# Idle products moved into TensorE's small gaps, and the third block's scores moved behind the sum over w1, in a gated cross-attention and feed-forward kernel

## The chip, the cores and the metric

The kernel runs on one core of a Trainium2 chip. The metric is the time of one execution on the device, in microseconds, lower is better; several runs are taken and their median is shown. A profile of one execution comes beside it, and its "span" runs from the first to the last instruction of that execution.

## The reference

Inputs are x (4 blocks of 512 rows of 512), a context ctx (4 blocks of 512 rows of 128), two gates, one attention vector W of 256 numbers with its bias b, and three weights of 1408 x 512 (w1, w2) and 512 x 1408 (w3).

```python
# attention part, per block
si = ctx @ W[:128];  sj = ctx @ W[128:]
att = 0.6 * sigmoid(si[:, None] + sj[None, :] + b) + 0.4 * layernorm(x)
x = x + tanh(g_xattn) * att
# feed-forward part, on layernorm(x)
bitlinear(v, w) = quant8(rmsnorm(v)) @ quant_ternary(w).T
x = x + tanh(g_ffn) * bitlinear(silu(bitlinear(h, w1)) * bitlinear(h, w2), w3)
```

`quant_ternary` divides a weight by the mean of its absolute values, rounds and clips to -1, 0, 1. So a weight can be rounded only when the sum of |w| over the whole weight is known. `quant8` scales each row by its largest absolute value.

## The kernel before

The 2048 rows are 16 tiles of 128 rows, numbered 0 to 15; a block (batch entry) has four of them. Each tile goes through: scores and tanh (attention), layer norm, rounding to 8 bits, a turn on TensorE (`pt`, line 419), the unloading of the turned tile (`un`, line 427 on ScalarE or 429 on VectorE), products with w1 (`G`, the gates, `pg` in the trace) and with w2 (`U`, `pu`), silu (`SI`), the product of both (`ST`), its largest value (`AM`), rounding, another turn, products with w3 (`D`, `po`), and the write.

Nothing schedules the work: the string `ORDER` (line 33) lists the steps, and each engine runs its own instructions in that order. An instruction that waits holds up all that follows on its engine. A digit after a step is its tile, block or weight, `.k` a part of it, and the last letter the engine (a ScalarE, v VectorE, p GpSimd). The steps that matter here:

- `bp2` and the like (`spread_param`, line 196): a one-row product that spreads a scalar over the partitions; `up` (line 202, 204) reads it. `bp1` spreads the attention gate, from whose tanh `cg` (line 217 to 222, VectorE) makes the constants that the layer norm scale needs.
- `pi b` (line 315): the row scores of block b, four products of one column, each with a load of its own; `si b` (line 327, ScalarE) reads them. `pj b` (line 322): the column scores, one product of 512 columns in 32-bit floats.
- `wu n` (`keep_busy`, line 180): n products of 128x512 whose result, the tile `idle`, nobody reads.
- `A1.k`, `A2.k`: sums of |w| of part k on ScalarE (line 242) or VectorE (line 244). `tot1`, `tot2` (line 248): TensorE adds the parts over the partitions. `M1`, `M2` (lines 253 to 256, VectorE): mean and its inverse. `R` (lines 264, 266): the weight is scaled and rounded; `C` (line 269): it is clipped into the f16 weight that the products read. The tiles between `R` and `C` have three buffers.
- The scores, `tot`, `pt` and the spread scalars all take turns in two PSUM buffers (`ps_o`, tag "po"), in program order: each new one waits until the one two places before it has been read.

At the start, in program order and before `ORDER` begins: DMAs of the parameters, constants (`ones`, `mhalf`, the identity), the tile `ones16` of ones on GpSimd, three idle products, and then `bc` (lines 185 and 186), which spreads W over the partitions and is copied to `wc` by ScalarE (line 188). The scores need `wc`.

Of the kernel before, what the change touches and what calls it, by code (L numbers as in the profile page):

```python
# [11 lines left out]
F16 = mybir.dt.float16  # L12
# [8 lines left out]
P = 128  # L21
# [11 lines left out]
ORDER = """  # L33
x0 ctx0 x3 x2 x1 ctx1 w1.0 w1.1 w1.2 w1.3 ctx2 ctx3 w2.0 w2.1 w2.2 w2.3 x10 w3.0 x4 x6 x8 w3.1 w3.2
x14 x12 st0 bp1 up1 cg cc st3 bp0 up0 pi0 si0 st2 pj0 th2 st1 la2 th0 la0 th1 pi1 lb2v at2 si1 lb0v
at0 ce0v at1 ce1v am0 an0 th3 at3 am1 an1 A1.0a A1.1a A1.2a wu4 bp2 pj1 up2 wu13 pi2 A1.3v pjs1 sq1
A1.4v si2 ce3p sq0 am3 tot1 M1 ce2p r1p r0p pt1 un1a R1.2v pt0 un0v R1.3a am2 an3 pi3 si3 an2 C1.3v
C1.2v A2.0a th7 pj2 R1.0p C1.0v A2.1a wu4 G0.0 R1.1p A2.2v A2.3a C1.1v A2.4v G1.0 G1.1 st10 tot2 M2
R2.0v G0.1 r2v sq3 sq2 r3p G0.2 G0.3 dq0 C2.0v R2.1p st11 st5 C2.1v pjs2 R2.2a C2.2v pt3 pj3 SI0
R2.3a C2.3v G1.2 lc0 G1.3 SI1 st4 st6 un3a th6 U0.0 th4 U0.1 U0.2 U0.3 ST0 U1.0 U1.1 st7 U1.2 U1.3  # L40
ST1 A3.1a dq2 pt2 un2a mr la4 lb4v th5 at4 G3.0 G3.1 G3.2 pjs3 G3.3 SI3 at5 ce5a at6 ce4v am5 G2.0
G2.1 G2.2 an5 G2.3 SI2 U3.0 U3.1 at7 am4 U3.2 ce6p an4 U3.3 ST3 ce7p U2.0 U2.1 r5p pt5 am7 sq4 sq6
an7 sq5 r4p sq7 un5a th8 r7p A3.0a am6 U2.2 U2.3 pt4 G5 ST2 st8 an6 st9 dq4 r6p AM1 AN1 th11 un4a
SI5 A3.2a U5 ST5 lc2 pt6 pt7 G4 th10 la8 lb8v at10 at8 un6a G6 at11 AM5 SI4 QU1p th9 fx3p ce10a
sq10 ce11p am11 an11 ce8p am8 an8 AN5 un7a U4 ST4 T1 r11p tot3 M3 AM2 SI6 am10 fx1p an10 AN2 sq11
W1a G7 at9 sq8 pt11 un11a SI7 r8p U6 SQ0 pt8 un8a U7 ST6 R3.1p ce9p SQ1 r10p pt10 sq9 am9 lc4 an9
os un10a ST7 st15 th15 r9p dq8 G8 SI8 th14 G11 SI11 AM0 R3.2p pt9 U8 th12 QU2p AN0 st14 st12 st13
QU0p C3.1v un9a ST8 G10 SQ7 AM8 la12 lb12v at14 th13 at13 G9 T0 ce13v SI10 AM6 lc8 fx2p R3.0a am13
an13 SI9 U11 ST11 AM7 AN7 SQ6 AM3 C3.0p T2 W2a U9 ST9 W0a AN3 at15 SQ2 ce14p r13p U10 pt13 un13a
AN6 am14 an14 C3.2p DQ0 D1 S1 QU7p at12 T7 sq14 W7a QU3p ce12v am12 ce15p SQ3 AN8 sq13 an12 am15  # L50
an15 SQ5 DQ2 G13 r15p fx7p ST10 D2 S2 SQ11 D0 sq12 fx8p AM11 fx0p S0 sq15 dq12 T3 QU6v r12p AN11
U13 W3a SI13 DQ6 lc12 ST13 fx13p QU8p pt15 r14p O2 D7 un15a S7 pt12 un12a SQ10 SQ8 AM4 G15 SI15 AN4
QU4p T6 W6v D3 S3 O3 QU5p fx9p O7 fx6p AM9 AN9 SQ13 fx14p D6 S6 T8 QU9p O1 AM10 AN10 AM13 SQ9 W8a
U15 ST15 AN13 SQ4 T5 G12 T4 fx12p W5a D5 W4a fx4a fx11p AM15 fx5a O0 fx10p SI12 DQ4 S5 DQ8 D8 S8 T9
W9a QU11p U12 ST12 AM12 O8 pt14 un14a AN12 T11 AN15 O6 QU13p O5 DQ10 W11a D4 S4 D9 fx15p T13 S9
QU12v SQ12 G14 W13a QU10v T12 W12v O9 D11 S11 D13 QU15v T10 SI14 DQ12 S13 U14 ST14 T15 AM14 AN14
SQ15 DQ15 W10a D10 S10 QU14v W15a O11 D12 S12 O12 SQ14 T14 W14a D15 DQ14 O10 O13 S15 D14 S14 O15 O4
O14
"""


# [1 line left out]
def flamingo_gated_kernel(  # L63
# [29 lines left out]
    act, dve, pool, pe, sp = nc.scalar, nc.vector, nc.gpsimd, nc.tensor, nc.sync  # L93

    const = ctx.enter_context(tc.tile_pool(name="const", bufs=1))
# [65 lines left out]
        load_param(i)  # L161


    ones = const.tile([P, P], F32, name="ones")
    dve.memset(ones, 1.0)
    mhalf = const.tile([P, TB], F32, name="mhalf")
# [4 lines left out]
    act.activation(warm, ones[:, 0:1], AF.Silu)  # L171


    ones16 = const.tile([P, 512], F16, name="ones16")
    pool.memset(ones16, 1.0)  # L175
    idle = ps_gu.tile([P, 3 * 512], F32, tag="gu", name="idle")

    def keep_busy(n):
        for _ in range(n):
            pe.matmul(idle[:, :512], ones16[:, :P], ones16, start=True, stop=True)  # L180


    keep_busy(3)
    bc = ps_o.tile([P, 512], F32, tag="po", name="bc")
    pe.matmul(bc[:, P : P + 1], row[:, :C], ones[0:1, 0:1], start=True, stop=True)
    pe.matmul(bc[:, :P], row[:, C : 2 * C], ones[0:1, :], start=True, stop=True)
    wc = const.tile([P, P + 1], F32, name="wc")
    act.activation(wc, bc[:, : P + 1], AF.Copy)
    wj, wi = wc[:, :P], wc[:, P : P + 1]
# [113 lines left out]
    am1 = const.tile(NTT, F32, name="am1")  # L303
# [267 lines left out]
    for step in ORDER.split():  # L571
        name, n, k, eng = re.fullmatch(r"([A-Za-z]+)(\d*)\.?(\d?)([apv]?)", step).groups()
# [46 lines left out]
```

## Time and profile before

| | us |
|---|---|
| median of 3 runs | 157.71 (157.62 to 158.26) |
| the profiled execution | 157.83 |
| its span | 156.1 |
| TensorE busy | 146.2 (94%) |
| VectorE busy | 126.9 (81%) |
| ScalarE busy | 118.6 (76%) |
| GpSimd busy | 97.4 (62%) |
| idle products (L180), busy | 9.0, in 24 products |

The profile has views: busy times by engine, the span in 40 slices with the granted TensorE clock, the chain of work that ended last, the groups of instructions, the waits, and the timeline of one engine. In a chain or timeline row the first number is the start in microseconds from the span's start, the second the length. A bracket at the end of a timeline row gives how long the engine stood idle just before it and what ended that. Each 32-bit product appears as two pairs of a load (PEld) and a product (PE), so the four products of `pi` are shown as x8.

### The profile page before, as it was taken

How to read it: one execution, taken by the hardware profiler on the slowest of the kernel's cores; microseconds unless marked ns; L12 is line 12 of the kernel's file. 1: busy time of each engine (PE TensorE's matmuls, PEld its weight loads, DVE VectorE, ACT ScalarE, POOL GpSimd, SP SyncE). 2: the span in 40 equal slices, each digit the busy share in tenths (PEclk: the TensorE clock that was granted, in tenths of full speed). 3: DMA queues.
4: the chain of work that ended last, by engine and by line, in shares of the span. 5: the costliest groups of instructions: out<-in, count | busy, mean ns of one | idle time of the engine just before them, and what ended most of it. 6: DMA issues, size and time to landing. Idle time of an engine off the chain costs nothing.

```text
span 156.1 us, 2167 instructions
## 1 busy us (share of the span) xinstructions
PE 146.2 (94%) x704; PEld 75.4 (48%) x704; DVE 126.9 (81%) x216; ACT 118.6 (76%) x164; POOL 97.4 (62%) x161
## 2 busy tenths in 40 slices
PE   5999969979999999999999999999999999999980
PEld 2853643535554545555455454545554545555330
DVE  1679599999999999999999999959699296748621
ACT  3269499999799999997999879689979583737300
POOL 6241569782366886589959888889998962130400
PEclk9999995999999999999999999999999999999999
DMA  4799999996000000000000000100600321010162
GB/s 118 278 425 412 432 411 421 422 404 249 1 0 0 6 0 0 0 0 0 0 4 0 0 0 0 69 4 0 247 24 0 123 79 70 1 67 0 64 249 90
DMA packets 6690, 18.21 MB, mean 117 GB/s; under 512 B 663, under 2 KB 664, under 8 KB 6424
## 3 DMA queue, kind: packets, MB, share of 16 engines
q1 hardware_dynamic: 6672, 18.09, 29.4%
q8 instruction: 5, 0.08, 0.2%
q14 instruction: 5, 0.04, 0.1%
q10 hardware_dynamic: 8, 0.00, 0.0%
HBM read 13.89 MB, written 4.19 MB: 116 GB/s over the span
## 4 chain that ended last, share of the span: by engine, by line
PE 68%; DVE 21%; ACT 3%; POOL 3%; issue 1%; DVEq 0%; POOLq 0%; ACTq 0%
PE pg L459 19%; PE pu L459 18%; PE po L526 15%; PE idle L180 5%; DVE hs L471 5%; DVE f_am L483 5%; PE pj L322 3%; PE pi L315 3%; DVE x L366 2%; PE qp L419 2%; DVE x L531 2%; DVE am L388 2%; ACT junk L396 1%; DVE q L411 1%; PE pt L419 1%
## 5 line engine op out<-in xcount | busy, mean ns | idle before, releaser
L459 PEld LDWEIGHTS <-ht 128*128 128x128 f16 x384 | 37.7, 99 | 38.5 <-issue 3.5
L459 PE MATMUL pu<-w2q,ht 128*128 128x512 f16 (+1 forms) x192 | 40.4, 362 | 1.1 <-DVE w2q L269 1.1
L459 PE MATMUL pg<-w1q,ht 128*128 128x512 f16 (+1 forms) x192 | 41.1, 367 | 0.0
L526 PE MATMUL po<-w3q,qt 128*128 128x512 f16 x176 | 39.4, 379 | 0.7 <-ACT ht L427 0.4
L471 DVE SCALAR_TENSOR_TENSOR hs<-pu,a,hs 128x1408 f32<-128x1408 f32 x16 | 26.8, 1676 | 6.3 <-PE pu L459 2.4
L427 ACT ACTIVATE qt<-qp 128x1536 f16<-128x1536 int8 x14 | 20.2, 1448 | 12.9 <-PE qp L419 12.7
L526 PEld LDWEIGHTS <-qt 128*128 128x128 f16 x176 | 17.2, 98 | 20.1 <-issue 1.0
L467 ACT ACTIVATE hs<-pg,a 128x1408 f32<-128x1408 f32 x16 | 22.8, 1426 | 4.5 <-POOL a L406 2.4
L483 DVE TENSOR_REDUCE f_am<-hs 128x1 f32<-128x1409 f32 x16 | 25.7, 1609 | 0.1
L491 ACT ACTIVATE junk<-hs 128x1408 bf16<-128x1408 f32 x16 | 22.0, 1375 | 0.1
L500 POOL TENSOR_SCALAR q<-hs,f_qs 128x1024 int8<-128x1024 f32 (+1 forms) x22 | 19.2, 888 | 1.1 <-DVE f_qs L488 0.6
L531 DVE SCALAR_TENSOR_TENSOR x<-po,f_dq,x 128x512 f32<-128x512 f32 x16 | 11.9, 746 | 9.7 <-PE po L526 8.4
L345 DVE BATCH_NORM_STATS2 st<-x 128x6 f32<-128x512 f32 x16 | 10.8, 675 | 3.1 <-DMA x<-in_x_dram 3.1
L382 POOL TENSOR_SCALAR th_all<-x,ysum 128x512 f32<-128x512 f32 x9 | 6.8, 761 | 10.1 <-DVE x L366 6.6
L366 DVE SCALAR_TENSOR_TENSOR x<-x,sc,th_all 128x512 f32<-128x512 f32 x16 | 12.3, 788 | 0.7 <-ACT th_all L338 0.3
L411 POOL TENSOR_SCALAR q<-th_all,qs 128x512 int8<-128x512 f32 x15 | 10.3, 689 | 3.3 <-PE pt L419 1.4
L374 POOL TENSOR_SCALAR x<-x,c_sig,sh 128x512 f32<-128x512 f32 x14 | 11.6, 833 | 0.1
L516 POOL TENSOR_SCALAR f_w<-f_ss,kap 128x2 f32<-128x2 f32 (+1 forms) x9 | 2.4, 268 | 14.2 <-ACT junk L491 13.6
L388 DVE TENSOR_REDUCE am<-th_all 128x1 f32<-128x513 f32 x16 | 10.8, 676 | 0.0
L180 PE MATMUL idle<-ones 128*128 128x512 f16 x24 | 9.0, 534 | 1.8 <-POOL ones L175 1.8
L396 ACT ACTIVATE junk<-th_all 128x512 bf16<-128x512 f32 x16 | 10.1, 628 | 0.7
L427 ACT ACTIVATE ht<-pt 128x512 f16<-128x512 int8 x15 | 8.8, 589 | 1.9 <-PE pt L419 1.8
(94 smaller groups left out, 182.1 us busy)
## 6 DMA issues: line engine op xcount, KB each, us to landing
out_dram<-x SPq DMA_DIRECT2D x16, 256.0 KB, 2.3
x<-in_x_dram SPq DMA_DIRECT2D x6, 512.0 KB, 13.1
hs<-in_w1t_dram SPq DMA_DIRECT2D x4, 704.0 KB, 6.7
hs<-in_w2t_dram SPq DMA_DIRECT2D x4, 704.0 KB, 11.6
w3f<-in_w3t_dram SPq DMA_DIRECT2D x2, 1024.0 KB, 14.9
x<-in_x_dram SPq DMA_DIRECT2D x4, 256.0 KB, 5.1
ctx<-in_ctx_t_dram SPq DMA_DIRECT2D x4, 256.0 KB, 7.3
w3f<-in_w3t_dram SPq DMA_DIRECT2D x1, 768.0 KB
```

The lines of the kernel that those rows point to most:

```text
L180: pe.matmul(idle[:, :512], ones16[:, :P], ones16, start=True, stop=True)
L366: dve.scalar_tensor_tensor(xt(n), xt(n), col(sc, n), ths[n], ALU.mult, ALU.add, accum_out=col(ysum, n))
L388: dve.tensor_reduce(col(am1, n), th_all[:, th_slot[n], : D + 1], AX.X, ALU.max, apply_absolute_value=True)
L427: act.activation(dst, src, AF.Copy)
L459: pe.matmul(gus[tag, n][:, c0 : c0 + cn], hts[n][:, kk, :], wq[:, kk, c0 : c0 + cn], start=(kk == 0), stop=(kk == ND - 1),)
L467: act.activation(tts[n], gus.pop(("pg", n))[:, :H], AF.Silu, scale=col(a1, n))
L471: dve.scalar_tensor_tensor(tts[n], gus.pop(("pu", n))[:, :H], col(a1, n), tts[n], ALU.mult, ALU.mult)
L483: dve.tensor_reduce(col(f_am, n), hs[:, t_slot[n], : H + 1], AX.X, ALU.max, apply_absolute_value=True)
L491: act.activation(junk[:, :H], tts[n], AF.Square, accum_out=col(f_ss, n))
L500: eng.tensor_scalar(dst, src, col(f_qs, n), 127.0, ALU.mult, ALU.mult)
L526: pe.matmul(po[:, :D], qt[:, f, :], w3q[:, f, :], start=(f == 0), stop=(f == NH - 1))
L531: dve.scalar_tensor_tensor(xt(n), pos.pop(n)[:, :D], col(f_dq, n), xt(n), ALU.mult, ALU.add)
```

## The change

1. The memset of `ones16` on GpSimd stands ahead of the other constants.
2. Four idle products ahead of `bc` where there were three, and three new ones between `bc` and `bp1`.
3. In `ORDER`: `wu13 pi2` ahead of `tot1` becomes `wu12`; `pi2` and `si2` go behind `pt0`; `wu2` stands between `pt1` and `pt0`, another `wu2` between `pt0` and `pi2`, `wu3` ahead of `pj2`, and the `wu4` ahead of `G0.0` becomes `wu2`.

```diff
-at0 ce0v at1 ce1v am0 an0 th3 at3 am1 an1 A1.0a A1.1a A1.2a wu4 bp2 pj1 up2 wu13 pi2 A1.3v pjs1 sq1
-A1.4v si2 ce3p sq0 am3 tot1 M1 ce2p r1p r0p pt1 un1a R1.2v pt0 un0v R1.3a am2 an3 pi3 si3 an2 C1.3v
-C1.2v A2.0a th7 pj2 R1.0p C1.0v A2.1a wu4 G0.0 R1.1p A2.2v A2.3a C1.1v A2.4v G1.0 G1.1 st10 tot2 M2
+at0 ce0v at1 ce1v am0 an0 th3 at3 am1 an1 A1.0a A1.1a A1.2a wu4 bp2 pj1 up2 A1.3v pjs1 sq1 A1.4v
+ce3p sq0 am3 wu12 tot1 M1 ce2p r1p r0p pt1 un1a R1.2v wu2 pt0 wu2 pi2 si2 un0v R1.3a am2 an3 pi3
+si3 an2 C1.3v C1.2v A2.0a th7 wu3 pj2 R1.0p C1.0v A2.1a wu2 G0.0 R1.1p A2.2v A2.3a C1.1v A2.4v G1.0
+G1.1 st10 tot2 M2
...
+    ones16 = const.tile([P, 512], F16, name="ones16")
+    pool.memset(ones16, 1.0)
     ones = const.tile([P, P], F32, name="ones")
...
-    ones16 = const.tile([P, 512], F16, name="ones16")
-    pool.memset(ones16, 1.0)
     idle = ps_gu.tile([P, 3 * 512], F32, tag="gu", name="idle")
...
-    keep_busy(3)
+    keep_busy(4)
     bc = ps_o.tile([P, 512], F32, tag="po", name="bc")
     pe.matmul(bc[:, P : P + 1], row[:, :C], ones[0:1, 0:1], start=True, stop=True)
     pe.matmul(bc[:, :P], row[:, C : 2 * C], ones[0:1, :], start=True, stop=True)
+    keep_busy(3)
```

All that follows `M2` in `ORDER` is as before. On TensorE the instructions otherwise keep their order; on ScalarE only `si2` moves, from ahead of `sq0` to behind `un1a`, just ahead of `R1.3a`; GpSimd has the memset of `ones16` ahead of the identity; VectorE and the DMA queue keep their order. With `pi2` moved, `tot1` and `pt1` take other PSUM buffers: `tot1` now waits for `up2`, `pt1` for `pjs1`, `pi2` for `un1a`, `pi3` for `un0v`, `pj2` for `si2`.

More of the change, by code (lines that the diff above doesn't have):

```diff
@@ L35 @@
 x14 x12 st0 bp1 up1 cg cc st3 bp0 up0 pi0 si0 st2 pj0 th2 st1 la2 th0 la0 th1 pi1 lb2v at2 si1 lb0v
-at0 ce0v at1 ce1v am0 an0 th3 at3 am1 an1 A1.0a A1.1a A1.2a wu4 bp2 pj1 up2 wu13 pi2 A1.3v pjs1 sq1
-A1.4v si2 ce3p sq0 am3 tot1 M1 ce2p r1p r0p pt1 un1a R1.2v pt0 un0v R1.3a am2 an3 pi3 si3 an2 C1.3v
-C1.2v A2.0a th7 pj2 R1.0p C1.0v A2.1a wu4 G0.0 R1.1p A2.2v A2.3a C1.1v A2.4v G1.0 G1.1 st10 tot2 M2
-R2.0v G0.1 r2v sq3 sq2 r3p G0.2 G0.3 dq0 C2.0v R2.1p st11 st5 C2.1v pjs2 R2.2a C2.2v pt3 pj3 SI0
@@ L40 @@
[L40 to L57, printed above, removed]
@@ L58 @@
-O14
+at0 ce0v at1 ce1v am0 an0 th3 at3 am1 an1 A1.0a A1.1a A1.2a wu4 bp2 pj1 up2 A1.3v pjs1 sq1 A1.4v
+ce3p sq0 am3 wu12 tot1 M1 ce2p r1p r0p pt1 un1a R1.2v wu2 pt0 wu2 pi2 si2 un0v R1.3a am2 an3 pi3
+si3 an2 C1.3v C1.2v A2.0a th7 wu3 pj2 R1.0p C1.0v A2.1a wu2 G0.0 R1.1p A2.2v A2.3a C1.1v A2.4v G1.0
+G1.1 st10 tot2 M2 R2.0v G0.1 r2v sq3 sq2 r3p G0.2 G0.3 dq0 C2.0v R2.1p st11 st5 C2.1v pjs2 R2.2a
+C2.2v pt3 pj3 SI0 R2.3a C2.3v G1.2 lc0 G1.3 SI1 st4 st6 un3a th6 U0.0 th4 U0.1 U0.2 U0.3 ST0 U1.0
+U1.1 st7 U1.2 U1.3 ST1 A3.1a dq2 pt2 un2a mr la4 lb4v th5 at4 G3.0 G3.1 G3.2 pjs3 G3.3 SI3 at5 ce5a
@@ new lines @@
+at6 ce4v am5 G2.0 G2.1 G2.2 an5 G2.3 SI2 U3.0 U3.1 at7 am4 U3.2 ce6p an4 U3.3 ST3 ce7p U2.0 U2.1
+r5p pt5 am7 sq4 sq6 an7 sq5 r4p sq7 un5a th8 r7p A3.0a am6 U2.2 U2.3 pt4 G5 ST2 st8 an6 st9 dq4 r6p
+AM1 AN1 th11 un4a SI5 A3.2a U5 ST5 lc2 pt6 pt7 G4 th10 la8 lb8v at10 at8 un6a G6 at11 AM5 SI4 QU1p
+th9 fx3p ce10a sq10 ce11p am11 an11 ce8p am8 an8 AN5 un7a U4 ST4 T1 r11p tot3 M3 AM2 SI6 am10 fx1p
+an10 AN2 sq11 W1a G7 at9 sq8 pt11 un11a SI7 r8p U6 SQ0 pt8 un8a U7 ST6 R3.1p ce9p SQ1 r10p pt10 sq9
@@ new lines @@
+am9 lc4 an9 os un10a ST7 st15 th15 r9p dq8 G8 SI8 th14 G11 SI11 AM0 R3.2p pt9 U8 th12 QU2p AN0 st14
+st12 st13 QU0p C3.1v un9a ST8 G10 SQ7 AM8 la12 lb12v at14 th13 at13 G9 T0 ce13v SI10 AM6 lc8 fx2p
+R3.0a am13 an13 SI9 U11 ST11 AM7 AN7 SQ6 AM3 C3.0p T2 W2a U9 ST9 W0a AN3 at15 SQ2 ce14p r13p U10
+pt13 un13a AN6 am14 an14 C3.2p DQ0 D1 S1 QU7p at12 T7 sq14 W7a QU3p ce12v am12 ce15p SQ3 AN8 sq13
+an12 am15 an15 SQ5 DQ2 G13 r15p fx7p ST10 D2 S2 SQ11 D0 sq12 fx8p AM11 fx0p S0 sq15 dq12 T3 QU6v
+r12p AN11 U13 W3a SI13 DQ6 lc12 ST13 fx13p QU8p pt15 r14p O2 D7 un15a S7 pt12 un12a SQ10 SQ8 AM4
@@ new lines @@
+G15 SI15 AN4 QU4p T6 W6v D3 S3 O3 QU5p fx9p O7 fx6p AM9 AN9 SQ13 fx14p D6 S6 T8 QU9p O1 AM10 AN10
+AM13 SQ9 W8a U15 ST15 AN13 SQ4 T5 G12 T4 fx12p W5a D5 W4a fx4a fx11p AM15 fx5a O0 fx10p SI12 DQ4 S5
+DQ8 D8 S8 T9 W9a QU11p U12 ST12 AM12 O8 pt14 un14a AN12 T11 AN15 O6 QU13p O5 DQ10 W11a D4 S4 D9
+fx15p T13 S9 QU12v SQ12 G14 W13a QU10v T12 W12v O9 D11 S11 D13 QU15v T10 SI14 DQ12 S13 U14 ST14 T15
+AM14 AN14 SQ15 DQ15 W10a D10 S10 QU14v W15a O11 D12 S12 O12 SQ14 T14 W14a D15 DQ14 O10 O13 S15 D14
+S14 O15 O4 O14
```

## The prediction

> **What bounds the kernel now.** I read the page's 40 slices first:
>
> ```profile
> PE   5999969979999999999999999999999999999980
> ```
>
> TensorE is at 9 tenths from slice 10 to slice 38 (39 us to near the end), so a shift of the first gates and ups moves all that follows. The change ends ahead of `M2`, so the question is when `M2` and the products behind it start. Next the chain of work that ended last:
>
> ```profile
> 1.82 1.46 PE idle L180 x3
> 3.28 0.51 PE bc L185 x2
> ...
> 5.49 1.84 PE pi L315 x8
> 7.32 1.92 PE pj L322 x2
> 9.24 1.50 PE pi L315 x8
> 10.74 1.73 PE idle L180 x4
> ...
> 14.98 3.62 PE idle L180 x13
> 18.60 0.80 PE pi L315 x8
> ...
> 27.80 0.13 PE tot L248 x2
> 27.93 0.02 issue
> 27.96 0.18 DVE mean L253
> ...
> 33.59 4.32 PE pu L459 x21
> ```
>
> The chain stays on TensorE almost without a break from 1.82 to 19.4. It reaches `tot2` at 27.80 and `M2` at 27.96, and from 33.59 on TensorE is dense again. Then VectorE's timeline, for what `tot1` releases:
>
> ```profile
> 19.65 0.16 DVE L253 TENSOR_REDUCE mean<-tot 128x1 f32<-128x5 f32 x1 [1.69 <-PE tot L248]
> ...
> 22.49 1.38 DVE L269 TENSOR_SCALAR w1q<-wk 128x1408 f16<-128x1408 int16 x3
> ```
>
> VectorE stood idle 1.69 us for `tot1` and was then busy without a break up to 27.86, where `st10` ends (27.68 + 0.18). So `M2` at 27.96 is 0.10 behind VectorE's own work: TensorE's path to `tot2` is late by that 0.10 and no more. Of this stretch the order on VectorE is the bound.
>
> Third, the clock. In the stretch table the granted clock is:
>
> ```profile
> 23.00:24.00 1.00, 1.00 (x4) 0.28 (x2) 1.00 (x4) 1.00 (x3) 0.90 (x1) 0.66 1.07 416
> ...
> 26.00:27.00 1.00, 1.00 (x5) 0.40 (x3) 1.00 (x3) 0.91 (x3) 0.92 (x2) 0.63 0.89 358
> ```
>
> 0.66 and 0.63 at a floor of 0.50 put the fall at 23.32 and the return at 26.73, 3.41 us apart. The page has no record for the first 16 us and prints 9 there, but the rows speak: `wu4` at 10.74 took 1.73, 0.43 a product; the starts inside `wu13` are 0.43 apart up to 16.48 and 0.22 apart after it. So TensorE ran at half speed until 16.49, at full speed for two steps of 3.41, at half speed for one. Steps fall at 9.66, 13.08, 16.49, 19.90, 23.32, 26.73. What went through the array in each (column streams of `pj` and idle products; `pi` and `bp` stream one column): 6.25 to 9.66 1.9 us, no rise; 9.66 to 13.08 1.8 us, no rise; 13.08 to 16.49 all 3.4, rise; 16.49 to 19.90 1.9, kept; 19.90 to 23.32 about 1.0 (`pj2` alone), fall. So a rise wants somewhere between 1.9 and 3.4 us of streaming in a step, and keeping wants between 1.0 and 1.9.
>
> [...]
>
> **The change, step by step** (times of the profiled execution).
>
> 1. *`ones16` first.* GpSimd's first memset of this set starts at 0.72 and `ones16` takes 0.52, so the idle products start at 1.29 and not 1.82: 0.53 gained, and the fourth costs 0.43. `bc` comes 0.10 earlier at 3.11, or not at all earlier if the parameter row lands later (its landing isn't shown). The identity is 0.5 later; its first reader is at 19.83, so nothing.
>
> 2. *`wu3` between `bc` and `bp1`.* `bp1` needs only the gate's DMA and ran at 4.23, in the shadow of the copy to `wc`; the hole was just 4.65 to 4.80. Now three products at half speed (0.43 each) start at 4.13. A one-row load comes 0.56 behind the last idle product's start (11.83 to 12.39 at `bp2`, 2.65 to 3.21 at `bc`), so `bp1` is at 4.98 + 0.56 = 5.54 and `bp0` 0.52 behind at 6.06, where it stood at 4.80. `pi0` starts at 6.58 instead of 5.49: **+1.1 us**. All behind it follows: `pj0`, the four tanh on ScalarE, `at2` on VectorE (10.06, it waited for the tanh), the sums A1. VectorE's gate constants are 1.4 later, its statistics 0.7; they are ready ahead of the tanh. The last A1 sum ends at 17.37 + 1.1 = 18.46. The weights don't hide this: VectorE's A1 sums were not waiting for a DMA.
>
> 3. *One idle product fewer, `pi2` out of the way.* `wu12` starts at 14.78 + 1.1 = 15.88. If the clock still rises at 16.49, the second product ends at 16.61 and ten more by 0.216 end at 18.77, which is when `tot1` starts: **0.48 earlier** than 19.25, and behind the A1 sums (18.46).
>
> 4. *`pi2` and `si2` behind `pt0`.* `pt1` starts 0.2 after `tot1` (18.97), `un1a` on ScalarE 0.37 after that (19.34) and takes 0.59. On TensorE two idle products, `pt0` and two more (0.43 + 0.13 + 0.43) put `pi2` at 20.10. From `pi2` to `si2` took 0.99 (18.43 to 19.42), so `si2` is at 21.09. Behind it on ScalarE waits `R1.3a`, which ran at 20.67 and now at 21.25; it takes 1.47, and `C1.3v` on VectorE can't start before 22.75. It was at 22.49: **+0.26**. VectorE's own order would have had it 0.48 earlier, at 22.0, so the gain of step 3 turns into a wait for `R1.3a`. Behind `C1.3v` are `C1.2v`, `C1.0v`, A2.2v, C1.1v, A2.4v, `st10` and `M2`, and GpSimd's `R1.1p`, which waits for a buffer that `C1.3v` frees: all +0.26. `st10` ends at 28.12.
>
> 5. *The pairs and the clock at 23.32.* Behind `pi2` (0.85) `pi3` waits for `un0v`, which VectorE ends at 21.30, and ends at 22.2; `wu3` ends at 22.85, then `pj2`. Streaming from 19.90 to 23.32 becomes 0.2 + 0.65 + 0.47 = 1.3 us against a need between 1.0 and 1.9: open. If the clock holds, `G1.1` waits for `C1.1v`, which ends at 26.4, and `tot2` is done by 27.2. If it falls, the rest of `pj2` and `wu2` end at 25.05 and `G0.0`, `G1.0` (1.17 each at half speed) and `G1.1` bring `tot2` to 27.8. Both are ahead of 28.12, where `st10` ends: TensorE is no longer what `M2` waits for, and the 0.10 by which `tot2` was late goes, of which 0.02 of issue stays: **-0.08**. Bounds: 0 and -0.10. The held clock itself buys nothing here; what runs at half speed until 26.73 had the wait for `C1.1v` as its cover. The price of the pairs is in step 4.
>
> Sum: +0.26 - 0.08 = **+0.18** at `M2`. `C2.0v` to `C2.3v` and `U0.1` at 33.59 hang on `M2` through VectorE, busy from there without a hole, so the shift goes through to the end: 157.83 + 0.18 = **158.0** us. The profiled execution is 0.12 above the median of the runs, inside their range.
>
> **The rivals.**
>
> *Late rise* (slower). The step from 13.08 to 16.49 now holds `bp2` (0.5 us without streaming) and, if 32-bit `pj` counts for less than a f16 product, only 0.9 us of sure streaming instead of 1.5. Without the rise at 16.49 it comes at 19.90: 9.4 of the twelve idle products run at 0.43, `tot1` starts at 20.46, 1.69 later than above: 158.0 + 1.7 = **159.7**. It decides as soon as that one step misses the mark. For it: the stretch with unbroken streaming starts 1.1 later, and steps 3.4 apart would miss it in 1.1/3.4, a third, of the cases, were they placed at random against the program (one profile cannot show whether they are). Against: the three us left are far over the 1.9 that failed.
>
> *Early rise* (faster). Seven idle products in the first 5.4 us: 1.29 to 2.98 and 4.13 to 5.41. A step that lies just over them holds 2.2 us, more than the 1.9 that failed. Then `pi0`, `pj0` and `pi1` (1.84, 1.92, 1.50) halve, the 1.1 is paid back, and VectorE goes by the gate constants, which `wu3` delays: some 0.4 late, A1 sums done at 17.75, `tot1` at 17.8, 0.97 before step 3's: **157.0**. Against: with steps at 2.84 and 6.25 as here, only 1.4 us fall into the step.
>
> *It doesn't do what it says.* The clock falls at 23.32 all the same (two of its three terms are idle products that may be too few): by step 5 the time stays 158.0, by its upper bound 158.1. The time doesn't tell it from the forecast, only the granted clock does.
>
> **How the numbers follow.** Forecast (start 1.1 late, rise at the same step, `R1.3a` behind `si2`) 0.49, with 157.7 to 158.6 as its own range, from TensorE's small steps of 0.1 to 0.2 in step 4 and from a `bc` that doesn't come earlier; late rise 0.26; early rise 0.17; something that I don't see, on either side, 0.08. The time is the forecast's, 158.0. The range reaches to both rivals, 156.9 to 159.8. Half a per cent, 0.8 us, is about what a measurement of this kernel tells from no change: faster than 156.9 is the lower part of the early rise and the unseen, 0.12; slower than 158.5 is the late rise, the forecast's top and the unseen, 0.34; between, 0.54.
>
> **What the profile after would show.** `bp1` near 5.5 and `pi0` near 6.6 (step 2); idle products 0.22 apart from 16.5 on or from another step (steps 3, rivals); `tot1` near 18.8; `si2` right ahead of `R1.3a` at about 21.2 and VectorE idle before `C1.3v` with ScalarE's rounding as its releaser (step 4); no stretch at 0.50 between 23 and 27 (step 5); `M2` near 28.1. I am wrong if the clock rises in the first 10 us, if the first scores are not late, or if VectorE doesn't stand before `C1.3v`.

## The result, and the profile after

| | before | changed |
|---|---|---|
| median of 19 runs each, us | 157.51 (156.62 to 158.88) | 158.20 (157.74 to 158.85) |
| ratio | | 1.0046, 95% interval 1.0025 to 1.0067 |
| profiled execution, us | 157.83 | 157.75 |
| its span, us | 156.1 | 156.0 |

The change costs about 0.7 us, clear of noise and just under half a per cent. The two profiled executions do not show it: that of before lies above the median of its runs, that of the changed kernel at the bottom of its own. Why the runs of the kernel before differ by 2 us is part of the answer below.

The chain of the changed kernel, start and length as before:

```profile
1.29 1.89 PE idle L180 x4
3.18 0.51 PE bc L185 x2
3.69 0.64 PE bc L186 x2
4.33 1.39 PE idle L180 x3
5.72 0.94 PE spread L197 x4
6.66 1.80 PE pi L316 x8
8.46 1.93 PE pj L323 x2
...
10.47 1.84 ACT th_all L339 x3
...
17.95 0.62 ACT junk L397 x2
18.57 0.09 issue
18.65 0.36 PE tot L249 x2
...
20.97 0.02 ACT si L328
20.99 0.14 issue
21.13 1.47 ACT wk L265
22.60 0.02 issue
22.62 1.40 DVE w1q L270 x3
...
27.82 0.18 DVE mv L347
28.01 0.06 DVE mean L254
...
33.52 4.32 PE pu L460 x21
```

The chain now leaves TensorE twice. From 10.39 to 18.65 it runs over ScalarE, through the tanh (`th_all`), the sums over w1 and the sums of squares (`junk` at 17.95): `tot1` at 18.65 no longer waits for the idle products. TensorE's timeline has it standing idle for 0.29 there:

```profile
18.65 0.36 PE L249 MATMUL tot<-acc,ones 128*128 128x5 f32 x2 [0.29 <-ACT junk L397]
```

Behind `pi2` it goes from `si2` on ScalarE (20.97) to the rounding `R1.3a` (`wk`, 21.13), to VectorE's clipping `C1.3v` (`w1q`, 22.62) and on along VectorE to `M2` at 28.01. The first scores (`pi`) start at 6.66 in the chain (6.59 in TensorE's timeline) behind three idle products and the spread scalars, where they started at 5.49. VectorE's timeline has the two places where a wait went and one came:

```profile
19.05 0.16 DVE L254 TENSOR_REDUCE mean<-tot 128x1 f32<-128x5 f32 x1
...
22.62 1.40 DVE L270 TENSOR_SCALAR w1q<-wk 128x1408 f16<-128x1408 int16 x3 [0.65 <-ACT wk L265]
```

In this execution there is no wait for `tot1` any more (it was 1.69), and 0.65 for ScalarE's rounding instead. The clock, from the table of stretches (the third number from the end of a row is the granted clock):

```profile
22.00:23.00 1.00, 1.00 (x5) 0.45 (x5) 0.38 (x1) 1.00 (x3) 0.00 (x0) 0.56 0.98 398
...
25.00:26.00 1.00, 1.00 (x5) 0.36 (x4) 1.00 (x2) 1.00 (x2) 0.91 (x2) 0.74 0.98 401
```

0.56 and 0.74 at a floor of 0.50 (the two stretches between show 0.50) put the fall at 22.12 and the return at 25.53. The pairs did not hold the clock in this execution.

In other executions it held. By an estimate, a step of 3.41 us at half speed takes 3.41 x 0.5 / 156 = 0.011 off the mean granted clock of a run, which is on record for all 19 runs of the changed kernel (the time ahead of the first rise has no record and does not count). Eleven runs have 0.993 or more, so no such step in them. They are the eleven slower ones, 158.11 to 158.85. The eight fastest, 157.74 to 157.87, have 0.987 to 0.989, as the profiled execution has. So a held clock did not make the kernel fast.

### The profile page after: what moved, and what is told of

It is laid out like the page before. It is cut to its first block, busy times and chain, and to the rows that moved or that the text cites. A ratio compares the mean times of both kernels' runs of the same rounds, so it can differ in the third digit from the quotient of the medians.

```text
span 156.0 us, 2183 instructions
## 1 busy us (share of the span) xinstructions
PE 147.7 (95%) x712; PEld 76.0 (49%) x712; DVE 126.8 (81%) x216; ACT 118.5 (76%) x164; POOL 97.4 (62%) x161
## 4 chain that ended last, share of the span: by engine, by line
PE 61%; DVE 25%; ACT 6%; issue 3%; POOL 3%; DVEq 0%; ACTq 0%; POOLq 0%
PE pu L460 18%; PE pg L460 17%; PE po L527 15%; DVE hs L472 5%; DVE f_am L484 5%; PE idle L180 3%; DVE x L367 2%; PE qp L420 2%; DVE x L532 2%; PE pi L316 2%; DVE am L389 2%; DVE acc L245 1%; DVE w1q L270 1%; ACT junk L397 1%; ACT junk L243 1%
## 5 line engine op out<-in xcount | busy, mean ns | idle before, releaser
L460 PE MATMUL pg<-w1q,ht 128*128 128x512 f16 (+1 forms) x192 | 40.3, 361 | 0.0
L180 PE MATMUL idle<-ones 128*128 128x512 f16 x32 | 11.3, 492 | 1.3 <-POOL ones L165 1.3
```

Source lines behind the costliest of these rows:

```text
L460: pe.matmul(gus[tag, n][:, c0 : c0 + cn], hts[n][:, kk, :], wq[:, kk, c0 : c0 + cn], start=(kk == 0), stop=(kk == ND - 1),)
```

## Experiments

Each kernel ran 6 to 19 times beside the kernel before on the same chip; the ratio is to that, and compares across the groups run together (e1 to e4, e5 to e8, e9 and e10), between which the median of before moved from 157.56 to 157.82 and 157.62. A price in us that stands with a ratio is the ratio's share of 157.5 us; the medians alone can lie further apart. "Rise" is where the clock reached full speed in the profiled execution, by the records of the granted clock; the columns behind it are start times in the same execution (`M1 to C1.3v` a distance), all in us.

| kernel | us, median | ratio to before, interval | rise | tot1 | M1 to C1.3v | M2 |
|---|---|---|---|---|---|---|
| before | 157.51 | 1 | 16.49 | 19.25 | 2.84 | 27.96 |
| changed | 158.20 | 1.0046 (1.0025 to 1.0067) | 15.29 | 18.65 | 3.57 | 27.92 |
| e1, no products behind `bc` | 157.02 | 0.9967 (0.9940 to 0.9994) | 16.37 | 18.44 | 3.58 | 27.64 |
| e2, before + these products | 158.82 | 1.0051 (1.0025 to 1.0076) | 17.10 | 20.17 | 2.85 | 28.89 |
| e3, `R1.3a` ahead of `si2` | 157.89 | 1.0013 (0.9992 to 1.0035) | 17.76 | 19.42 | 2.85 | 28.00 |
| e4, both mended | 156.85 | 0.9946 (0.9921 to 0.9971) | 16.40 | 18.32 | 2.85 | 26.91 |
| e5, e4 with `wu6` | 156.58 | 0.9906 (0.9878 to 0.9933) | 15.13 | 17.52 | 2.85 | 26.75 |
| e6, e4 without pairs | 157.01 | 0.9948 (0.9922 to 0.9974) | 16.41 | 18.44 | 2.84 | 27.16 |
| e7, changed, no pairs around `pt0` | 158.07 | 1.0018 (0.9998 to 1.0039) | 17.13 | 19.11 | 3.56 | 28.29 |
| e8, e4 with one product at the start | 156.81 | 0.9935 (0.9912 to 0.9957) | 14.32 | 17.68 | 2.85 | 26.90 |
| e9, e5 without late idle products | 156.21 | 0.9919 (0.9890 to 0.9949) | 14.32 | 17.37 | 2.84 | 26.03 |
| e10, e9 without any idle product | 158.89 | 1.0095 (1.0057 to 1.0132) | 27.91 | 17.34 | 2.84 | 28.39 |

Theory: the change delays the first gates in two places, at the three products behind `bc` and at `si2` ahead of `R1.3a`. Rivals: the pairs themselves cost; the early products pay for themselves through the clock; all is the place of the clock step.

**e1.** The changed kernel without the three products.

```diff
-    keep_busy(3)
     wc = const.tile([P, P + 1], F32, name="wc")
```

> The changed kernel without the three idle products between bc and the gate's spread (the fourth idle product ahead of bc stays). Theory (two delays: the three products put the first scores 1.1 us later; si2 ahead of the rounding R1.3a holds the clipping C1.3v): row scores of block 0 back at 5.4 us, last sum over w1 done at 17.4 us, tot1 0.5 to 1.1 us earlier than in the changed kernel at the same place of the clock step, C1.3v still 3.97 us behind tot1. Time about 157.6 us, 0.5 us under the changed kernel, about level with the kernel before. Rival (the pairs in the gaps carry the cost): stays at 158.2 us.

Measured 157.02, ratio 0.9967, lower than both sides expected. The pairs alone are not the cost. The last A1 sum ended at 17.93 and not at 17.4: in this execution `pi0` waited 0.77 us for the DMA of the first context block and started at 6.04. In the kernel before this transfer landed at about 5.4 (issued at 1.2, 4.2 us to its landing), just ahead of `pi0`'s first load at 5.46; it is the next limit at the start, and e4 (0.50 us) and e6 (0.72 us) wait for it too.

**e2.** The kernel before with the three products alone.

```diff
+    keep_busy(3)
     wc = const.tile([P, P + 1], F32, name="wc")
```

> The kernel before with only the three idle products between bc and the gate's spread. Theory: row scores of block 0 at 6.8 us, last sum over w1 done at 18.6 us, tot1 later by 1.1 us on average over the places of the clock step, and nothing behind it to give that back: 158.3 to 158.7 us, 0.8 to 1.1 us over the kernel before. Rival (the pairs in the gaps carry the cost): 157.5 us, as before. Second rival (early products raise the clock early and pay for themselves): under 157.5 us with the granted clock at 1.00 before 10 us.

158.82, ratio 1.0051: 0.8 us for this one edit by the ratio (the medians lie 1.3 us apart), `pi0` at 6.69. The clock rose at 17.10 in the profiled execution, so it did not rise early. Its profile shows the wait for `tot1` as before, now to 20.57:

```profile
20.57 0.16 DVE L254 TENSOR_REDUCE mean<-tot 128x1 f32<-128x5 f32 x1 [1.37 <-PE tot L249]
...
23.42 1.38 DVE L270 TENSOR_SCALAR w1q<-wk 128x1408 f16<-128x1408 int16 x3
```

**e3.** The changed kernel with two steps swapped.

```diff
-wu2 pi2 si2 un0v R1.3a am2
+wu2 pi2 un0v R1.3a si2 am2
```

> The changed kernel with R1.3a ahead of si2 on ScalarE, nothing else. Theory: R1.3a starts right behind un1a, C1.3v follows tot1 by 3.24 us again and not by 3.97 us, and VectorE does not wait there; 0.5 to 0.7 us under the changed kernel, about 157.5 us. Rival (the late start alone carries the cost, the wait for R1.3a is covered): 158.2 us.

157.89, ratio 1.0013. The mechanism is as expected: `C1.3v` starts 2.85 us after `M1` (3.57 in the changed kernel), with no wait in the row:

```profile
19.74 0.16 DVE L254 TENSOR_REDUCE mean<-tot 128x1 f32<-128x5 f32 x1 [0.64 <-PE tot L249]
...
22.59 1.38 DVE L270 TENSOR_SCALAR w1q<-wk 128x1408 f16<-128x1408 int16 x3
```

The size, 0.33% or 0.5 us by the two ratios, is at the lower end; the intervals of the two kernels overlap a little, so the time alone would not settle it.

**e4.** The edits of e1 and e3 together.

```diff
-    keep_busy(3)
     wc = const.tile([P, P + 1], F32, name="wc")
...
-wu2 pi2 si2 un0v R1.3a am2
+wu2 pi2 un0v R1.3a si2 am2
```

> The changed kernel without the three products behind bc and with R1.3a ahead of si2. Theory: both delays gone, what is left of the change is one idle product fewer and pi2 out of the way of tot1: tot1 0.6 to 1.0 us earlier than before, C1.3v 3.24 us behind it, 156.7 to 157.0 us, under both kernels by 0.5 us or more. Rival (the time depends only on where the clock step falls): level with the kernel before, 157.5 us, with the same spread.

156.85, ratio 0.9946: under both kernels, as expected, and with runs from 156.57 to 157.22 only. The rival that time hangs on the clock step alone falls: e4 rose at 16.40, before at 16.49, and its `tot1` is 0.93 earlier.

Together, e1 to e4 give the price of each delay with and without the other, as differences of ratios. The three products cost 0.0079 (changed to e1) and 0.0067 (e3 to e4), so 1.2 and 1.1 us. The order on ScalarE costs 0.0033 (changed to e3) and 0.0021 (e1 to e4), so 0.5 and 0.3 us, and here the intervals of the two kernels overlap each time. What is left of the change, e4, gains 0.0054, or 0.85 us.

**e7.** The changed kernel without the pairs on either side of `pt0`.

```diff
-R1.2v wu2 pt0 wu2 pi2 si2
+R1.2v pt0 pi2 si2
```

> The changed kernel without the two pairs between pt1 and pi2; the three behind bc stay and si2 stays ahead of R1.3a. Theory (the order on ScalarE is the delay, not the 0.43 us of two idle products): pi2 then waits for un1a instead, si2 comes 0.1 to 0.3 us earlier at most, 158.0 to 158.2 us. Rival (the pairs are what pushes si2 and R1.3a back): C1.3v follows tot1 by 3.3 us or less, 157.7 us or less.

158.07, as expected, and the wait is unmoved:

```profile
19.43 0.16 DVE L254 TENSOR_REDUCE mean<-tot 128x1 f32<-128x5 f32 x1 [0.33 <-PE tot L249]
...
22.99 1.40 DVE L270 TENSOR_SCALAR w1q<-wk 128x1408 f16<-128x1408 int16 x3 [0.63 <-ACT wk L265]
```

0.63 us behind ScalarE without the pairs, 0.65 with them. `pi2` then waits for `un1a`. With e3, it is the order on ScalarE, `si2` ahead of `R1.3a`, and not the idle products, that delays `C1.3v`.

**e6.** e4 without the pairs, the three ahead of `pj2` and the two ahead of `G0.0`.

```diff
-R1.2v wu2 pt0 wu2 pi2
+R1.2v pt0 pi2
...
-th7 wu3 pj2 R1.0p C1.0v A2.1a wu2 G0.0
+th7 pj2 R1.0p C1.0v A2.1a G0.0
```

> The version with both delays gone, without the pairs and the three in the gaps (between pt1 and pt0, between pt0 and pi2, ahead of pj2, ahead of G0.0). Theory (the held clock buys nothing, since the gates wait for C1.1v): the clock falls to 0.50 for one step of 3.41 us between 20 and 28 us, M2 stays behind st10 on VectorE, time 156.8 to 157.0 us as with the pairs. Rival (the pairs pay by holding the clock): 157.3 us or more.

157.01, ratio 0.9948 against 0.9946 with them: they are worth nothing that can be told. The clock fell for 23.24 to 26.65 and `tot2` came 0.19 after VectorE was ready for it.

**e8.** e4 with one product at the start in place of four.

```diff
-    keep_busy(4)
+    keep_busy(1)
```

> The version with both delays gone, with one idle product at the start in place of four. Theory (the products at the start are too few to raise the clock and pay nothing; the scores wait for bc or for the DMA of the first context block): clock rises at the same kind of place as before, 13.5 to 18 us, time 156.6 to 156.9 us. Rival (they carry part of the warming): clock rises a step later in some runs, time 157.2 us or more.

156.81, ratio 0.9935, rise at 14.32: the products at the start pay nothing that can be told. Its profile shows one thing more:

```profile
26.90 0.16 DVE L253 TENSOR_REDUCE mean<-tot 128x1 f32<-128x5 f32 x1 [0.61 <-PE tot L248]
```

`M2` is where e4 has it (26.91), though `tot1` came 0.64 earlier than in e4: `M2` waits 0.61 for `tot2`. So with both delays gone an early `tot1` runs into TensorE's way to `tot2`. That fits the small price of the order between e1 and e4.

**e5.** e4 with six idle products ahead of `tot1`.

```diff
-ce3p sq0 am3 wu12 tot1
+ce3p sq0 am3 wu6 tot1
```

> The version with both delays gone (no products behind bc, R1.3a ahead of si2) with six idle products ahead of tot1 in place of twelve. Theory (tot1 waits for the run of idle products, whose length hangs on where the clock step falls): at half speed six end ahead of the last sum over w1 (17.7 us), so tot1 is at 17.7 to 17.8 us wherever the step falls, 0.6 us earlier than with twelve, and the runs lie closer together: 156.3 to 156.5 us, spread under 0.5 us. Rival (the run of twelve pays by raising the clock): the clock rises a step of 3.41 us later, the first gates run at half speed and the time is 157 us or more.

156.58, ratio 0.9906, just above the time expected, with a spread of 0.70 where under 0.5 was expected. `tot1` came at 17.52, when its sums were there; the rival (a later rise) did not occur here, 15.13. But only two of six runs were near 156.0, the rest at 156.6, and the profile of one of the latter shows what bounds it:

```profile
26.75 0.16 DVE L253 TENSOR_REDUCE mean<-tot 128x1 f32<-128x5 f32 x1 [0.62 <-PE tot L248]
```

`M2` now waits 0.62 for `tot2`: with the first half mended, TensorE's way through `pj2`, idle products and gates, at half speed from 21.96 to 25.37, is the bound. The clock alone does not tell the two kinds of run apart: by their mean granted clock of 0.995 it held in the two faster ones, but by 0.996 and 0.997 it held in two of the slower ones too.

**e9.** e5 without the idle products ahead of `pj2` and `G0.0`.

```diff
-th7 wu3 pj2 R1.0p C1.0v A2.1a wu2 G0.0
+th7 pj2 R1.0p C1.0v A2.1a G0.0
```

> The version with six idle products ahead of tot1, without the three ahead of pj2 and the two ahead of G0.0 (the pairs around pt0 stay). Theory (with tot1 at 17.5, M2 waits 0.6 us for tot2, and the idle products that run at half speed ahead of pj2 and G0.0, 1.3 and 0.9 us, are what TensorE spends there): tot2 is done before st10, M2 starts at 26.1 to 26.2 right behind st10, 156.0 to 156.2 us. Rival (without them the clock falls for longer and the gates take the time back): M2 at 26.7 or later, 156.5 us or more.

156.21, ratio 0.9919, `M2` at 26.03 though the clock fell at 21.14. `tot2` was expected ahead of `st10` and came at about the same time. What it waits for is ScalarE's last sum over w2, by the chain of this kernel:

```profile
24.67 0.89 ACT junk L242 x2
25.56 0.04 issue
25.61 0.40 PE tot L248 x2
26.00 0.02 issue
26.03 0.17 DVE mean L253
```

It has the lowest median of all, 156.21, and is 0.8% under the kernel before. By the ratios it is not told apart from e5 (0.9906), so the gain over e5 rests on the place of `M2` in two profiles and not on the times.

**e10.** The same without any idle product.

```diff
-    keep_busy(4)
...
-A1.2a wu4 bp2
+A1.2a bp2
...
-am3 wu6 tot1
+am3 tot1
...
-R1.2v wu2 pt0 wu2 pi2
+R1.2v pt0 pi2
```

> The same without any idle product anywhere. Theory (idle products pay only through the clock in the scores and the first gates, and cost nothing once tot1 no longer waits for them): the clock rises only with the first gates, near 28 to 31 us; the scores pi2, pi3 and pj2 run at half speed, about 2 us more on TensorE's way to tot2, tot2 at 27.5 to 28.5, and G0.1 to G1.3 partly at half speed ahead of U0: 157 to 159 us. Rival (idle products are worth nothing at all): 156.0 to 156.3 us, as without the late ones.

158.89, ratio 1.0095. `pi2` and `pi3` take 1.86 each where they took 0.95 and 1.05, the first gates run at half speed up to the rise at 27.91 (nine products from 24.69 on take 3.54 us, the nine from 28.21 on 1.94), and VectorE stands:

```profile
28.39 0.16 DVE L252 TENSOR_REDUCE mean<-tot 128x1 f32<-128x5 f32 x1 [2.24 <-PE tot L247]
```

2.24 us for `tot2`. So the idle products of e9, with which the first rise came at 14.32, are worth 2.7 us by the medians (ratios 1.0095 and 0.9919). Of those that the change added, the pairs and the three ahead of `pj2` (e6) and the fourth at the start (e8) are worth nothing that can be told, and the three behind `bc` cost time.

## Why the prediction was right, and where its size was off

- *The time.* That 158.0 came within 0.2 of 158.20 is in part luck. The sum foresaw +0.18 and started from an execution 0.32 above what became the median of 19 runs; measured against measured the change is +0.69. The range, 156.9 to 159.8, took in both rivals.
- *What bounds.* Right. `M2` followed `st10` on VectorE (`mv` at 27.82 for 0.18 us, `M2` on the chain from 28.01; its row in the timeline, and in the table, starts at 27.92), and the shift there went through to the end. The term for `tot2`, -0.08 with bounds 0 and -0.10, was too small: `M2` starts 5.30 behind `C1.3v` where it started 5.47 behind it, -0.17.
- *Step 1.* Right: idle products from 1.29, `bc` at 3.11 as worked out.
- *Step 2, the three products.* Right in mechanism and size: `bp1` at 5.65 for 5.54, `pi0` at 6.59 for 6.58, last A1 sum at 18.51 for 18.46. e1 and e2 price it at 0.8 to 1.2 us of the whole time (0.0079 between the changed kernel and e1, 0.0051 between e2 and before).
- *Step 4, `si2` ahead of `R1.3a`.* Right: `si2` at 20.97 for 21.09, `R1.3a` at 21.13 for 21.25, `C1.3v` at 22.62 for 22.75, each 0.12 early because `tot1` was (18.65 for 18.77). That `tot1` fell so close is luck: the rise came at 15.29 and not at 16.49, and `tot1` waited for the sums and not for the idle products. The distance from `tot1` to `C1.3v` is no luck: 3.97, as the sum had it. e3 and e7 show that the order does it.
- *Step 3, the term that was mis-sized.* The prediction put `tot1` 0.48 earlier, "if the clock still rises at 16.49", the place in the one profile of before. The rise isn't at one place. Three kernels with the same program up to `tot1`, the changed one, e3 and e7, rose at 15.29, 17.76 and 17.13; over the eleven profiles with idle products it lies between 14.32 and 17.76, 3.44 us (column "rise"). So the two kernels must be compared over the places. The three kernels have their `tot1` at 18.65, 19.42 and 19.11: half a microsecond per microsecond between the last two, and a floor at 18.65, where the last A1 sum has ended (18.51) and TensorE stood idle 0.29.

  In the kernel before the run of streaming starts 1.1 us earlier, so by an estimate, over all places, its rises should lie 1.1 us earlier too, worth 0.55 in `tot1`. That takes back the 0.48: the average gain of step 3 is about nothing. This is worked out and not shown, as only one profile of before was taken. Two things on record agree with it. e4, which has the gain of step 3 without the two delays, is 0.85 us under before, while the sum had step 3 make good the late start of 1.1 and 0.48 besides, 1.58 in all. And the mean granted clocks tell where the fastest runs of before rose, by an estimate: the two fastest of those run beside e1 to e4, 156.57 and 156.82, have 0.987 over spans of 154.8 and 155.0, so about 4.0 us at half speed, one step of 3.41 and 0.5 to 0.8 at the end; the profile's last fall comes 139.95 behind its rise (156.44 and 16.49), which puts the rise of these runs between 14.1 and 14.6, against 16.49 in the profiled execution of 157.83.

  Left is `M2`, which moved 0.56 away from `M1` (8.87 for 8.31): 0.73 between `M1` and `C1.3v` (3.57 for 2.84) less the 0.17 above. Measured is 0.69, with an interval from 0.39 to 1.06. The ends of the runs fit as well. By its products (13 at 0.216 from about 14.5, then 0.82 for `pi2`) the `tot1` of before would stand at about 18.2 for a rise at 14.3, an estimate; that is 0.5 under the floor of the changed kernel, and with the 0.56 makes about 1.0 between the fastest runs, which are 1.12 apart (156.62 and 157.74). And 8 of the 19 runs of the changed kernel lie within 0.13 of its fastest, as with a floor.
- *Step 5.* The streaming in the step that decides was 1.3 us in the prediction; at the place that came it was two pairs, 0.9 us, and the clock fell. The sign "no stretch at 0.50 between 23 and 27" failed in the profiled execution, and held in at least the eleven runs whose mean clock leaves no room for such a step. That the held clock buys nothing was right: e6, and those eleven runs are the slower ones. Where `tot1` comes earlier (e5, e8) `M2` does wait 0.6 us for TensorE, so the cover that the prediction named has an end.
- *The rivals.* Late rise: the hole of `bp2` that it named did not stop the rise in the profiled execution; the step from 11.88 to 15.29 held all of it (0.5 us) and the clock rose. The part that holds is the later start: the slowest run, 158.85, is 0.8 under its 159.7. Early rise: not seen in any profile, the earliest rise is 14.32, in kernels without the three products; and no run of the changed kernel came near its 157.0.

## What to carry to other kernels

Ahead of an engine that runs in order, a filler is free only where the engine waits for something that comes later than the filler ends: the hole at `bc` was 0.15 us and the filler, three products of 0.43, took 1.28. When a step is moved on one engine, look at what its reader pushes back on the next engine: `pi2` behind `pt0` was harmless on TensorE, its reader `si2` ahead of `R1.3a` was not. And where the clock's steps fall differently in each execution (rises from 14.32 to 17.76 here), a sum made at the place of one profile is a sample: compare the kernels over the places, by floors and slopes.

## What the runs showed of the hardware

- The changes of the granted clock came at 16.49, 23.32, 26.73 and 156.44 in the profile of before and at 15.29, 22.12, 25.53 and 155.24 in that of the changed kernel: 6.83, 3.41 and 129.71 us apart in both, 2, 1 and 38 times 3.413. Their place against the program differed between executions: with the same program up to `tot1` the rise came at 15.29, 17.76 and 17.13 (changed kernel, e3, e7), and the twelve idle products ahead of `tot1` took 2.75, 3.67 and 3.36 us. The runs of before, in which `tot1` waits for such a run of products, spread by 2.3 us. In e4 they spread by 0.65 us; what evens them out may be the wait for `tot2` that e8 shows, but no run tests that.
- The 3.41 us ahead of the rise held about 2.8 us of streaming and a hole of 0.5 to 0.6 us with a one-row product in the changed kernel (rise at 15.29) and in e8 and e9 (14.32). In before the 3.41 us from 6.25 to 9.66 held 1.9 us, and the idle products from 10.74 on still took 0.43 each. These sums are estimates from start times.
- In e7 the clock stayed at full speed (mean granted clock 1.00) behind 3.41 us with 1.4 us of streaming (20.54 to 23.96: 0.64 of idle products and 0.75 of `pj2`); in e1 it fell behind 1.3 us (19.78 to 23.19: 0.64 and 0.68). These sums too are estimates from start times, and leave out one-column products. In the changed kernel it fell at 22.12 although TensorE's longest wait in the 3.41 us before was 0.31 us.
